# Aggregates scattered by row index where they are stored, and three sorts of single nodes moved from the last stage into the pair loop

## The chip, the cores and the metric

The kernel runs on one core of a Trainium2 chip (trn2). The metric is device time in microseconds (us), the median of the runs timed. A profile is one execution of its own; engines are called PE (TensorE, matrix products), DVE (VectorE), ACT (ScalarE), POOL (GpSimd) and SP (SyncE, which here only issues DMAs). L1380 is line 1380 of the kernel before.

## What is computed

Sixteen graphs of 1024 nodes with 64 channels go through two layers. Layer 0, after a layer norm and a ReLU, removes some edges of each node (by their rank) and takes, over the neighbours left and for each channel by itself, three quantiles; their weighted sum is the node's aggregate. A two-layer perceptron and a residual follow. Layer 1 is three graph convolutions with the full adjacency and a last linear layer. The part that matters here, cut:

```python
nd = adj_d > 0                                    # neighbours left, with the node itself
vals = jnp.where(nd[..., None], x[:, None, :, :], jnp.inf)
s = jnp.sort(vals, axis=2)
nv = nd.sum(2)
for tau, w in zip(TAUS, WTS):                     # 0.25, 0.5, 0.75
    pos = tau * jnp.maximum(nv - 1, 0)
    ...
    agg = agg + w * (v_lo + frac * (v_hi - v_lo))
out = x + agg
h = relu(out @ W1 + b1);  y = h @ W2 + b2          # layer 0
...
x1 = bn(relu(adj @ (h @ W) + b))                   # layer 1, three times
```

## The kernel before

**Pairs.** Graphs go in eight pairs; graph x of pair p is 2p + x. Rows of the tiles are the 64 channels of both graphs, or 128 nodes.

**Places.** `prepare_one` computes a graph's edges left and the number of neighbours of each node. Nodes are ranked by that number: `place` (L906) holds for every node its rank, so that nodes with few neighbours come first and one sorting network of fixed size serves a whole range of places. Rows of edges are sent to DRAM at their place by eight indirect DMAs of POOL (L914, `live_d`) and loaded back in that order (L929, `lp`). `find_live` and `list_rows` make from them what the sorts need.

**Two kinds of sort.** Places 0 to 639 (three blocks), 960 to 1007 (MID) and 1008 to 1023 (TAIL) are gathered by PE (`gather_block`: masks `s` made by DVE at L1170 or L1235, products at L1195 or L1266, ACT takes them out of PSUM) and sorted with channels on partitions. Places 640 to 959 are the single nodes (`NODES`, kinds 0, 1 and 2, with 17, 19 and 21 slots): `fetch_nodes` has POOL ask for each slot's rows with an indirect DMA (L1380, two per slot), and `sort_nodes` sorts them with nodes on partitions. Every sort is a network of DVE minima and maxima (L1111), then products (L1123) and sums (L1132). A sort of kinds 0 and 1 is for the two graphs of one pair, one of kind 2 for two pairs. `NODE_ORDER` lists the 20 sorts; `fetch_next` takes the next one of it and gives its rows a buffer (`gn` if nothing else is said). An ask waits for the DVE instruction that stood last in the program when it was written (L1387).

**Storing.** An aggregate of a block is turned by PE (L1292), copied by ACT into `o` (two buffers) and sent to `agg_d` of its graph at its places by ACT's DMA queue (L1302). One of single nodes is sent by SP's queue (L1426, L1429). `send` and `send_nodes` do this for what is waiting.

**Order.** `weave` interleaves, by hand-set shares, a sort with the steps of other generators. Each turn p of the pair loop (L1789) sorts pair p while `prepare` of pair p + 1 goes on (`SHARES`: how many of its steps go to each sort of the turn): block 0, a sort of single nodes, block 1, block 2, a second sort of single nodes, the MID places, and in turn 4 the TAIL places of four pairs. So 14 of the 20 sorts of single nodes are done in the loop's seven turns. The last pair is sorted in the late stage (L1821), with the six that are left, and there the steps of `later` are woven in (`LATE_SHARES`): for each pair, the rest of layer 0 (`first_layer`) and layer 1 (`next_layer`), the next pair's `first` between the steps of this pair's `second`. `done.sent` is the number of pairs whose aggregates are on their way.

**Loading.** `later` needs aggregates by node, while `agg_d` holds them by place. So `load` gathers them with sixteen indirect DMAs of POOL per pair (L1573), one per 128 nodes of each graph, by `place`. They go ahead of other work as the scheduler sees it (`high_priority`), but on POOL's queue instructions run in the order in which they stand. The tile `agg` is a single buffer. DVE's first instruction on it is L1470.

Of the kernel before, what the change touches and what calls it, by code (L numbers as in the profile page):

```python
# [14 lines left out]
I32 = mybir.dt.int32  # L15
# [17 lines left out]
SHARES = (20, 22, 14, 30, 9)  # L33
LATE_SHARES = (8, 8, 8, 8, 9, 9, 10, 8, 11, 8, 8)
# [11 lines left out]
    ((0,), 0), ((0,), 1), ((1,), 0), ((1,), 1), ((0, 1), 2), ((2,), 0), ((2,), 1), ((3,), 0), ((3,), 1), ((2, 3), 2),  # L46
    ((4,), 0), ((4,), 1), ((5,), 0), ((5,), 1), ((4, 5), 2), ((6,), 0), ((6,), 1), ((6, 7), 2), ((7,), 0), ((7,), 1),
# [27 lines left out]
REST = 960  # L75

# [332 lines left out]
def graph_layers_kernel(ctx: ExitStack, tc: tile.TileContext, ins, out: bass.AP):  # L409
# [80 lines left out]
    nc.gpsimd.iota(node_i, pattern=[[P, NT]], base=0, channel_multiplier=1)  # L490
    node = const.tile([P, NT], F32, name="node")
# [141 lines left out]
    agg_d = [dram.tile([N, C], F32, name=f"agg_d{b}") for b in range(NB)]  # L633
    live_d = [dram.tile([N, N // 4], I32, name=f"live_d{b}") for b in range(NB)]
# [149 lines left out]
    def prepare_one(st, x, pools, ahead=None):  # L784
# [5 lines left out]
        edge = work.tile([P, NT, N], F8, tag="byte", bufs=4, name="edge")  # L790
# [8 lines left out]
        for t in range(NT):  # L799
            a, coming = coming, load(t + 1) if t + 1 < NT else None  # L800
            nc.scalar.activation(  # L801
                edge[:, t, :], a[:, :].bitcast(U32), AF.Sign, accum_out=found[:, 0, b, t : t + 1], saturate=False
            )
            one = work.tile([P, N], F8, tag="one", bufs=2, name="one")
            nc.vector.tensor_scalar(one, a, 1.0, None, ALU.is_equal, saturate=False)  # L805
            pt = ps.tile([P, NT, P], F32, tag="big", bufs=2, name="ptE")
            for u in range(NT):
                nc.tensor.matmul(  # L808
                    out=pt[:, u, :], lhsT=one[:, u * P : (u + 1) * P], rhs=ident_h, start=True, stop=True
                )  # L810
            nc.scalar.activation(  # L811
                edgeT[:, :, t * P : (t + 1) * P], pt, AF.Copy, accum_out=found[:, 1, b, t : t + 1], saturate=False
            )
            yield
# [48 lines left out]
        for t in range(NT):  # L863
            q = ps.tile([P, N], F32, tag="big", bufs=2, name="q")
            for hf in range(NH):
# [19 lines left out]
                edge[:, t, :], q, AF.Relu, bias=bias(-2.0), accum_out=nv[:, t : t + 1], saturate=False  # L885
# [4 lines left out]
        nc.vector.scalar_tensor_tensor(key, nv, float(N), node, ALU.mult, ALU.add)  # L890
        minus = work.tile([P, NT], F32, tag="minus", name="minus")
# [32 lines left out]
        def fetch():  # L924

            lp = work.tile([P, NT, N // 4], I32, tag="byte", bufs=4, name="lp")
            for t in range(0, NT, 4):
                with tc.high_priority():
                    load = nc.gpsimd.dma_start(  # L929
                        out=lp[:, t : t + 4, :],  # L930
                        in_=live_d[b][t * P : (t + 4) * P, :].rearrange("(t p) n -> p t n", p=P),
                    )
                for sent in rows_sent:
                    tc.add_manual_dep(
                        load.ins, sent.ins.name,
                        mybir.DependencyInfo(mybir.DependencyClass.Sync, mybir.DependencyReason.DATA),
                        reason="rows sent by place",
                    )
            return lp[:, :, :].bitcast(F8)

        def find_live(lp_all, listed):
# [12 lines left out]

            half = slice(x * C, (x + 1) * C)
# [330 lines left out]

    def store(p, agg, cols, place0, pools, after=None):
# [13 lines left out]
        for x in range(2):  # L1301
            nc.scalar.dma_start(out=agg_d[2 * p + x][place0 : place0 + n, :], in_=o[:n, x * C : (x + 1) * C])  # L1302
# [64 lines left out]
    def fetch_nodes(pairs, i, pools, tag):  # L1367
# [4 lines left out]
        pool = work if tag == "s" else keep if tag == "r0" else rows  # L1372
        g = pool.tile([P, slots, G * C], F32, tag=tag, bufs=2 if tag == "s" else 1, name="g_nodes")
# [45 lines left out]
    def send_nodes():  # L1419

        for pairs, i, agg in waiting_nodes:
            j0, j1, _, _ = NODES[i]
            for a in range(agg.shape[1] // C):
                cols = slice(a * C, (a + 1) * C)
                if i < 2:
                    nc.sync.dma_start(out=agg_d[2 * pairs[0].p + a][j0:j1, :], in_=agg[:, cols])  # L1426
                else:
                    for x in range(2):
                        nc.sync.dma_start(  # L1429
                            out=agg_d[2 * pairs[a].p + x][j0:j1, :], in_=agg[x * C : (x + 1) * C, cols]  # L1430
                        )
# [124 lines left out]
    def later(pools, keep, done):  # L1556
# [4 lines left out]
        def load(p):  # L1561
# [5 lines left out]
            for x in range(2):  # L1567
# [3 lines left out]
                with tc.high_priority():  # L1571
                    for t in range(NT):
                        nc.gpsimd.indirect_dma_start(  # L1573
                            out=agg[:, t, x, :],
                            out_offset=None,
                            in_=agg_d[b][:, :],
                            in_offset=bass.IndirectOffsetOnAxis(ap=place[:, b, t : t + 1], axis=0),
                        )
# [184 lines left out]
    with ExitStack() as stack:  # L1763
# [6 lines left out]
        with ExitStack() as inner:  # L1770
# [18 lines left out]
            for p in range(NP - 1):  # L1789
# [3 lines left out]
                def steps(n):  # L1793
                    return ahead, SHARES[n], 0.0, 1.0

                weave(sort_block(st, 0, pools), gather_block(st, 1, pools), asking(nodes, 0.0, 0.9), steps(0))
                weave(sort_nodes(nodes, pools), gather_block(st, 2, pools), steps(1))
                nodes = fetch_next()
                weave(sort_block(st, 1, pools), asking(nodes, 0.1, 1.0, 0.4), steps(2))
                send_nodes()  # L1800
                both = rows_of_pairs(MID, p, p + 1, p, pools, "g1")
                weave(
                    sort_block(st, 2, pools), gather_block(st, MID, pools, into=both),
                    gather_block(st, MID + 1, pools, (early[0], "a", 2)), asking(nodes, 0.0, 0.7), steps(3),
                )
                if p in TAILS:
                    tails = rows_of_pairs(MID + 1, *TAILS[p], TAILS[p][1], pools, "g0")
                weave(sort_nodes(nodes, pools), steps(4))
# [12 lines left out]
        with ExitStack() as inner:  # L1821
# [5 lines left out]
            def steps(n):  # L1827
# [6 lines left out]
            then = [fetch_next("r0")]  # L1834
            weave(sort_block(st, 1, pools), asking(nodes, 0.0, 0.9), steps(2))
            send_nodes()
            both = rows_of_pairs(MID, NP - 1, NP, NP - 1, pools, "g1")
            weave(
                sort_block(st, 2, pools), gather_block(st, MID, pools, into=both), asking(then[0], 0.0, 0.9), steps(3)
            )  # L1840
            tails = rows_of_pairs(MID + 1, *TAILS[NP - 1], NP - 1, pools, "g0")
            weave(sort_nodes(nodes, pools), gather_block(st, MID + 1, pools, into=tails[:, :, -TW:]), steps(4))
            then += [fetch_next(), fetch_next("s"), fetch_next("s")]
            weave(
                sort_pairs(MID + 1, *TAILS[NP - 1], tails, pools), asking(then[1], 0.0, 0.5), asking(then[2], 0.5, 1.0),
                steps(5),
            )
            send(pools)
            done.sent = NP - 2
            weave(sort_nodes(then[0], pools), asking(then[3], 0.0, 1.0), steps(6))  # L1850
            send_nodes()
            weave(sort_pairs(MID, NP - 1, NP, both, pools), steps(7))
            send(pools)
            weave(sort_nodes(then[1], pools), steps(8))
            send_nodes()
            done.sent = NP - 1
            weave(sort_nodes(then[2], pools), steps(9))
            send_nodes()
            weave(sort_nodes(then[3], pools), steps(10))
# [52 lines left out]
```

## Time and profile before

| what | value |
|---|---|
| timed runs, median of 3 (lowest, highest) | 3202.37 us (3199.89, 3215.75) |
| the profiled execution's own time | 2820.77 us |
| its span, first to last instruction | 2819.0 us |
| mean granted clock of PE | 0.871 |
| preparation of the first pair | 0 to 213.7 us |
| pair loop, seven turns | 213.7 to 1995.1 us |
| late stage | 1995.1 to 2819.0 us |
| POOL, asks for rows of single nodes (L1380) | 744, 968.6 us busy |
| POOL, gathers of aggregates (L1573) | 128, 134.0 us busy |
| POOL, scatters of edge rows (L914) | 128, 178.3 us busy |

A row of a group of instructions reads: line, engine, operation, output<-inputs, shapes, count | busy us, mean ns of one | idle time of the engine just before them and what ended most of it. Durations come from the profiled execution, which is 382 us shorter than the median of the timed runs.

### The profile page before, as it was taken

Reading aid. Unit: us, or ns where it says so; the run is one execution under the profiler, and the core shown is the slowest. Engines: PE = TensorE matmul, PEld = TensorE weight load, DVE = VectorE, ACT = ScalarE, POOL = GpSimd, SP = SyncE. Lnnn points to the kernel's source line nnn. Section 1 sums busy time; section 2 is a strip of 40 time slices with the busy share of each in tenths; the row PEclk is TensorE's granted clock in tenths of the full one; section 3 lists DMA queues with packets and bytes.
Section 4 is the critical chain, followed back from the end, with each engine's and each line's share of the span. In section 5 each row is a group of like instructions: output and inputs, shape, how many; then the busy total and the mean of one; then the engine's idle time right before and its main releaser. Section 6 shows DMA issues by size and latency. Waiting matters only on the chain. (4 is left out here: it accounts for less than half of the span.)

```text
span 2819.0 us, 54552 instructions
## 1 busy us (share of the span) xinstructions
PE 2124.0 (75%) x21226; PEld 1366.3 (48%) x21226; DVE 2260.5 (80%) x5356; ACT 1660.1 (59%) x3325; POOL 1359.1 (48%) x1171
## 2 busy tenths in 40 slices
PE   3658976996898699779746986997689496448868
PEld 2435554563555466455524553654355363234445
DVE  3137998999999899989999999999688486647943
ACT  4795877678587768868673777687423141122222
POOL 7125554375345427534625274175636748852220
PEclk9779998997998899699978987998798798778989
DMA  4214222232422323242521322322311251221211
GB/s 128 75 49 124 76 71 73 87 91 64 117 74 72 77 83 92 55 124 59 106 46 47 94 86 64 112 76 64 81 19 30 65 83 52 43 58 43 53 52 47
DMA packets 261483, 205.28 MB, mean 73 GB/s; under 512 B 217568, under 2 KB 217696, under 8 KB 257120
## 3 DMA queue, kind: packets, MB, share of 16 engines
q1 hardware_dynamic: 169216, 131.76, 15.9%
q0 software_dynamic: 40192, 62.24, 9.1%
q10 hardware_dynamic: 51808, 7.71, 2.0%
q8 instruction: 168, 2.75, 0.4%
q14 instruction: 99, 0.81, 0.1%
HBM read 148.82 MB, written 52.75 MB: 72 GB/s over the span
## 5 line engine op out<-in xcount | busy, mean ns | idle before, releaser
L1380 POOL DMA_INDIRECT g_nodes<-rows_d,rows_listed x744 | 968.6, 1302 | 951.7 <-DVE prod L1123 282.6
L1195 PE MATMUL pg<-s,hp 128*64 128x496 fp8e4 (+5 forms) x8064 | 742.2, 335 | 128.9 <-ACT hp L716 47.4
L1195 PEld LDWEIGHTS <-hp 128*64 128x64 bf16 x8064 | 445.1, 113 | 370.4 <-ACT hp L716 67.5
L1528 PE MATMUL pg<-adjT,xw 128*64 128x512 fp8e4 x2304 | 280.9, 393 | 22.9 <-ACT xw L1517 12.4
L914 POOL DMA_INDIRECT live_d<-edge,place x128 | 178.3, 1393 | 162.2 <-DVE place L906 125.9
L1170 DVE TENSOR_SCALAR s<-r 128x3200 uint16<-128x3200 uint16 (+2 forms) x192 | 199.4, 1048 | 44.5 <-PE pg L1195 44.3
L1573 POOL DMA_INDIRECT agg<-agg_d,place x128 | 134.0, 1047 | 197.1 <-DMA agg_d<-agg_nodes 117.3
L1528 PEld LDWEIGHTS <-xw 128*64 128x64 bf16 x2304 | 135.2, 113 | 151.5 <-issue 21.6
L1199 ACT ACTIVATE g<-pg 128x400 f32<-128x400 f32 (+3 forms) x168 | 84.2, 501 | 183.4 <-PE pg L1195 153.4
L801 ACT ACTIVATE edge<-a 128x1024 fp8e4<-128x1024 uint32 x128 | 135.5, 1060 | 93.0 <-DMA a<-in_adj 92.4
L1111 DVE TENSOR_TENSOR t<-g 128x800 f32<-128x800 f32 (+9 forms) x184 | 168.3, 928 | 2.1
L884 ACT ACTIVATE edge<-q,bias 128x1024 fp8e4<-128x1024 f32 x128 | 142.2, 1112 | 42.6 <-PE q L879 42.6
L903 ACT ACTIVATE stays<-keys,minus 128x1024 fp8e4<-128x1024 f32 x128 | 143.7, 1123 | 39.0 <-PE keys L895 34.9
L857 ACT ACTIVATE stays<-cs,back 128x1024 f16<-128x1024 f32 x128 | 138.8, 1114 | 47.3 <-DVE look L838 28.7
L1111 DVE TENSOR_TENSOR g<-t 128x992 f32<-128x992 f32 (+7 forms) x176 | 160.0, 934 | 2.3
L949 PE MATMUL pt<-ident_h,lp 128*128 128x128 bf16 x1024 | 106.3, 273 | 61.9 <-ACT liveT L952 36.2
L1470 DVE TENSOR_TENSOR agg<-agg,h_late 128x1024 f32<-128x1024 f32 x8 | 9.8, 1230 | 177.1 <-DMA agg<-agg_d,place 177.1
L1266 PE MATMUL pg<-s,hp 128*64 128x384 bf16 (+14 forms) x1872 | 149.2, 301 | 2.6 <-DVE s L1235 2.6
L808 PE MATMUL ptE<-ident_h,one 128*128 128x128 bf16 x1024 | 83.2, 231 | 78.5 <-DVE one L805 43.8
L811 ACT ACTIVATE edgeT<-ptE 128x1024 fp8e4<-128x1024 f32 x128 | 130.5, 1030 | 16.3 <-PE ptE L808 14.5
L1532 ACT ACTIVATE xT<-pg,c_L_gnn_b 128x512 f32<-128x512 f32 x48 | 32.9, 686 | 181.5 <-PE pg L1528 173.3
L805 DVE TENSOR_SCALAR one<-a 128x1024 fp8e4<-128x1024 f32 x128 | 89.5, 704 | 53.9 <-DMA a<-in_adj 42.6
(255 smaller groups left out, 5067.7 us busy)
## 6 DMA issues: line engine op xcount, KB each, us to landing
a<-in_adj SPq DMA_DIRECT2D x128, 512.0 KB
adjT_d<-edgeT SPq DMA_DIRECT2D x16, 1024.0 KB
lp<-live_d POOLq DMA_DIRECT2D x32, 512.0 KB
adjT<-adjT_d SPq DMA_DIRECT2D x16, 1024.0 KB
g_nodes<-rows_d,rows_listed POOLq DMA_INDIRECT x744
room<-in_x SPq DMA_DIRECT2D x16, 256.0 KB
h_d<-room SPq DMA_DIRECT2D x16, 256.0 KB
rows_d<-room SPq DMA_DIRECT2D x64, 64.0 KB
```

Of the source, the lines that this page charges most:

```text
L801: nc.scalar.activation(edge[:, t, :], a[:, :].bitcast(U32), AF.Sign, accum_out=found[:, 0, b, t : t + 1], saturate=False)
L857: nc.scalar.activation(stays[:, t, :], cs, AF.Abs, bias=back[:, t : t + 1], scale=2.0)
L884: nc.scalar.activation(edge[:, t, :], q, AF.Relu, bias=bias(-2.0), accum_out=nv[:, t : t + 1], saturate=False)
L903: nc.scalar.activation(junk, keys, AF.Sign, bias=minus[:, t : t + 1], accum_out=above[:, t : t + 1], saturate=False)
L914: sent = nc.gpsimd.indirect_dma_start(out=live_d[b][:, :], out_offset=bass.IndirectOffsetOnAxis(ap=place[:, b, t : t + 1], axis=0), in_=ed ...
L1111: sorted_by[0] = nc.vector.tensor_tensor(view(bufs, o, n1, n2), view(bufs, a, n1, n2), view(bufs, b, n1, n2), ALU.max if op else ALU.min)
L1170: nc.vector.tensor_scalar(s[:, j, :, us, :], st.r[0][:, :, us, j0:j1], abs(k - 3), 0x0808, ALU.logical_shift_right if k > 3 else ALU.logic ...
L1195: summed = nc.tensor.matmul(out=pg[x * C : (x + 1) * C, those, :], lhsT=st.hp[:, part, x, u, :], rhs=picked, start=(i == 0 and part == 0), ...
L1266: summed = nc.tensor.matmul(out=pg[x * C : (x + 1) * C, ks, w0:], lhsT=st.hp[:, part, x, u, :], rhs=s[:, ks, x, u, w0:], start=(whole and ...
L1380: asked = nc.gpsimd.indirect_dma_start(out=g[:, k, a * C : (a + 1) * C], out_offset=None, in_=rows_d[st.p][:, :], in_offset=bass.IndirectO ...
L1528: nc.tensor.matmul(out=pg[cs, :], lhsT=part[:, u, cs], rhs=adjT[x][:, u, sl], start=(u == 0 and k == 0), stop=(u == NT - 1 and k == len(xw ...
L1573: nc.gpsimd.indirect_dma_start(out=agg[:, t, x, :], out_offset=None, in_=agg_d[b][:, :], in_offset=bass.IndirectOffsetOnAxis(ap=place[:, b ...
```

## The change

**Scatter.** Four bytes are added to each row of edges: the number of the node in the pair (0 to 2047, `own_row`). They travel with the row to its place, so that after loading, `node_of` holds for each place the node that has it; three small SP DMAs per graph bring the numbers of places 896 to 959, 960 to 1007 and 1008 to 1023 to partitions where they are wanted. `agg_d` is now one tensor for a pair, by node. All stores of aggregates are indirect DMAs of POOL (`scatter`), 19 a pair: two for each stored block, two for each sort of kind 0 or 1, and one per pair for kind 2. Different scatters of a pair do not wait for each other. `load` fetches `agg` with two plain SP DMAs, which wait for all scatters of that pair.

**Order of the sorts.** Turns 1, 3 and 5 of the loop have a third sort of single nodes. Its rows have the buffer `g1`, free once block 1 is sorted, and are asked for during the sort of block 2; in these turns the MID and TAIL places are gathered beside the last sort of single nodes rather than beside block 2. The late stage keeps three of the six: kind 2 of pairs 6 and 7, and kinds 0 and 1 of pair 7. `SHARES`, `LATE_SHARES` and `NODE_ORDER` follow. `done.sent` becomes 7 once the TAIL places are stored.

```diff
-SHARES = (20, 22, 14, 30, 9)
-LATE_SHARES = (8, 8, 8, 8, 9, 9, 10, 8, 11, 8, 8)
+SHARES = ((20, 22, 14, 0, 30, 9), (20, 22, 14, 16, 14, 9))
+LATE_SHARES = (6, 6, 8, 8, 6, 16, 8, 7)
 NODE_ORDER = (
-    ((0,), 0), ((0,), 1), ((1,), 0), ((1,), 1), ((0, 1), 2), ((2,), 0), ((2,), 1), ((3,), 0), ((3,), 1), ((2, 3), 2),
-    ((4,), 0), ((4,), 1), ((5,), 0), ((5,), 1), ((4, 5), 2), ((6,), 0), ((6,), 1), ((6, 7), 2), ((7,), 0), ((7,), 1),
+    ((0,), 0), ((0,), 1), ((0, 1), 2), ((1,), 0), ((1,), 1), ((2,), 0), ((2,), 1), ((2, 3), 2), ((3,), 0), ((3,), 1),
+    ((4,), 0), ((4,), 1), ((4, 5), 2), ((5,), 0), ((5,), 1), ((6,), 0), ((6,), 1), ((6, 7), 2), ((7,), 0), ((7,), 1),
 )
...
-    agg_d = [dram.tile([N, C], F32, name=f"agg_d{b}") for b in range(NB)]
-    live_d = [dram.tile([N, N // 4], I32, name=f"live_d{b}") for b in range(NB)]
+    agg_d = [dram.tile([2 * N, C], F32, name=f"agg_d{p}") for p in range(NP)]
+    live_d = [dram.tile([N, N // 4 + 1], I32, name=f"live_d{b}") for b in range(NB)]
...
+        nc.vector.tensor_copy(edge[:, :, N:].bitcast(I32), own_row[:, x, :, None])
...
+            nc.vector.tensor_copy(node_of[:, b, :NT, None], lp_all[:, :, N:].bitcast(I32))
+            for to, first, end in (
+                (nodes_of[x * C : (x + 1) * C, st.p : st.p + 1], 0, C),
+                (node_of[: MID_END - REST, b, NT : NT + 1], C, C + MID_END - REST),
+                (node_of[: N - MID_END, b, NT + 1 :], C + MID_END - REST, P),
+            ):
+                nc.sync.dma_start(out=to, in_=node_of[first:end, b, NT - 1 : NT])
...
+    def scatter(p, rows, data):
+
+        sent = nc.gpsimd.indirect_dma_start(
+            out=agg_d[p][:, :], out_offset=bass.IndirectOffsetOnAxis(ap=rows, axis=0), in_=data, in_offset=None
+        )
+        for other in agg_sent[p]:
+            tc.declare_no_dep(sent.ins, other.ins, reason="aggregates of different nodes")
+        agg_sent[p].append(sent)
...
         for x in range(2):
-            nc.scalar.dma_start(out=agg_d[2 * p + x][place0 : place0 + n, :], in_=o[:n, x * C : (x + 1) * C])
+            at = place0 // P + (place0 >= REST) + (place0 >= MID_END)
+            scatter(p, node_of[:n, 2 * p + x, at : at + 1], o[:n, x * C : (x + 1) * C])
...
-                    nc.sync.dma_start(out=agg_d[2 * pairs[0].p + a][j0:j1, :], in_=agg[:, cols])
+                    b = 2 * pairs[0].p + a
+                    scatter(pairs[0].p, node_of[:, b, j0 // P : j0 // P + 1], agg[:, cols])
...
-                with tc.high_priority():
-                    for t in range(NT):
-                        nc.gpsimd.indirect_dma_start(
-                            out=agg[:, t, x, :],
-                            out_offset=None,
-                            in_=agg_d[b][:, :],
-                            in_offset=bass.IndirectOffsetOnAxis(ap=place[:, b, t : t + 1], axis=0),
-                        )
+                load = nc.sync.dma_start(out=agg[:, :, x, :], in_=rows_of(agg_d[p][x * N : (x + 1) * N, :]))
+                for sent in agg_sent[p]:
+                    tc.add_manual_dep(
+                        load.ins, sent.ins.name,
+                        mybir.DependencyInfo(mybir.DependencyClass.Sync, mybir.DependencyReason.DATA),
+                        reason="aggregates of all nodes",
+                    )
...
                 weave(sort_nodes(nodes, pools), gather_block(st, 2, pools), steps(1))
+                more = fetch_next("g1") if p % 2 else None
                 nodes = fetch_next()
                 weave(sort_block(st, 1, pools), asking(nodes, 0.1, 1.0, 0.4), steps(2))
                 send_nodes()
+                if more is not None:
+                    weave(
+                        sort_block(st, 2, pools), asking(more, 0.0, 0.9), asking(nodes, 0.1, 0.9, 0.2), steps(3)
+                    )
+                    weave(sort_nodes(more, pools), asking(nodes, 0.0, 0.8), steps(4))
+                    send_nodes()
                 both = rows_of_pairs(MID, p, p + 1, p, pools, "g1")
-                weave(
-                    sort_block(st, 2, pools), gather_block(st, MID, pools, into=both),
-                    gather_block(st, MID + 1, pools, (early[0], "a", 2)), asking(nodes, 0.0, 0.7), steps(3),
+                small = (
+                    gather_block(st, MID, pools, into=both), gather_block(st, MID + 1, pools, (early[0], "a", 2)),
                 )
+                if more is None:
+                    weave(sort_block(st, 2, pools), *small, asking(nodes, 0.0, 0.7), steps(4))
+                    small = ()
...
-                weave(sort_nodes(nodes, pools), steps(4))
+                weave(sort_nodes(nodes, pools), *small, steps(5))
...
-            then += [fetch_next(), fetch_next("s"), fetch_next("s")]
-            weave(
-                sort_pairs(MID + 1, *TAILS[NP - 1], tails, pools), asking(then[1], 0.0, 0.5), asking(then[2], 0.5, 1.0),
-                steps(5),
-            )
+            weave(sort_pairs(MID + 1, *TAILS[NP - 1], tails, pools), steps(5))
             send(pools)
-            done.sent = NP - 2
-            weave(sort_nodes(then[0], pools), asking(then[3], 0.0, 1.0), steps(6))
+            done.sent = NP - 1
+            weave(sort_nodes(then, pools), steps(6))
             send_nodes()
             weave(sort_pairs(MID, NP - 1, NP, both, pools), steps(7))
-            send(pools)
-            weave(sort_nodes(then[1], pools), steps(8))
-            send_nodes()
-            done.sent = NP - 1
-            weave(sort_nodes(then[2], pools), steps(9))
-            send_nodes()
-            weave(sort_nodes(then[3], pools), steps(10))
             send(pools)
```

## Prediction, on record before the result

> **What bounds the kernel now.** I read the page's rows of busy time first, then busy time in chosen stretches, then the waits of each engine, then the order of time on GpSimd (POOL).
>
> The page's first part; then, from the answer on stretches, two of the seven turns of the pair loop and the late stage (the loop's first and last turns begin and end where `hp` is finished; columns: length, then busy us and count of PE, PEld, DVE, ACT, POOL, then granted clock, DMA share, GB/s):
>
> ```profile
> PE 2124.0 (75%) x21226; PEld 1366.3 (48%) x21226; DVE 2260.5 (80%) x5356; ACT 1660.1 (59%) x3325; POOL 1359.1 (48%) x1171
> ```
>
> ```profile
> 720.00:970.00 250.00, 202.81 (x2236) 132.40 (x2232) 237.13 (x537) 188.70 (x385) 120.18 (x93) 0.90 0.29 83
> 970.00:1220.00 250.00, 209.54 (x2220) 134.62 (x2218) 228.46 (x533) 185.33 (x366) 113.99 (x92) 0.87 0.28 82
> ...
> 1995.10:2819.00 823.90, 587.86 (x4815) 368.95 (x4815) 534.36 (x1107) 201.82 (x448) 396.78 (x329) 0.84 0.24 52
> ```
>
> There are two regimes. In a loop turn (213.7 to 1995.1, seven turns of 254 us) VectorE is busy 228 to 237 of 250 us: it is the bound, TensorE next with 203 to 210. In the late stage nothing is: of 824 us DVE works 534, PE 588. The waits of that stage say why:
>
> ```profile
> DVE agg L1470 <- DMA agg<-agg_d,place: 177.1, 8, 59.3
> ...
> POOL agg L1573 <- DMA agg_d<-agg_nodes: 117.3, 2, 59.2
> ```
>
> Eight times, once a pair, VectorE stands at L1470 until the gather of the aggregates has landed, 177.1 us in all. POOL in order of time at the longest of them (DVE's last earlier instruction began at 2440.05, L1470 at 2499.59) shows that the DMA's data were not what was late:
>
> ```profile
> 2474.58 0.95 POOL L1380 DMA_INDIRECT g_nodes<-rows_d,rows_listed  x1 [0.30 <-issue]
> 2475.83 0.94 POOL L1380 DMA_INDIRECT g_nodes<-rows_d,rows_listed  x1 [0.30 <-issue]
> 2477.08 0.95 POOL L1380 DMA_INDIRECT g_nodes<-rows_d,rows_listed  x1 [0.30 <-issue]
> 2478.33 0.95 POOL L1573 DMA_INDIRECT agg<-agg_d,place  x1 [0.30 <-issue]
> ...
> 2497.10 0.94 POOL L1573 DMA_INDIRECT agg<-agg_d,place  x1 [0.30 <-DMA agg<-agg_d,place]
> ```
>
> (The reader is to see a queue without a pause: one instruction every 1.25 us, first node rows asked for, then sixteen gathers, 20 us of issue in themselves.) POOL's queue, not its data, holds up VectorE, and with it TensorE, whose granted clock fell to 0.69 in the stretch 2417 to 2515.
>
> **Removed: the gathers.** The 128 at L1573 and the node rows queued ahead of them leave that path. `agg` comes by two SP DMAs a pair. SP issues the like of it (`xt<-in_x`) in 0.4 to 3.0 us, median 0.9, and its data wait on nothing but the free tile (the same wait as now) and the scatters of that pair. For pairs 0 to 3 these were sent long before, for 5 and 6 while pair 4 is worked on. Pairs 4 and 7 may still wait: tails sorted late, eight scatters of 1.25 us and a landing of about 2.4 us (the last gather of the final chain took 2.37), some 12 us for pair 4 if nothing covered it. I leave 12 us of the 177: -165. Bounds: -177 and -100 (if SP's waits in order give a third back).
>
> **Moved: three node sorts** (pairs 4 and 5 with kind 2, pair 6 with kinds 0 and 1 drop out of the late stage; by the new order one more sort falls into turns 1, 3 and 5). The late stage has two sorts of each kind, so half of its rows is one of each. The eight L1111 groups on `t_nodes` and `g_nodes` there are 39.2, 33.4, 22.3, 18.4, 17.3, 16.6, 12.5 and 10.3: 170.0 us for 318 instructions. The product rows are 6.3 + 4.9 + 2.4 + 1.7 = 15.3 us. Half is 92.7 us busy, less the 0.08 us by which neighbours overlap (0.28 long, 0.20 apart) on some 172 instructions: 79 us.
>
> Out of the late stage they are not worth 79. Without its stalls it is 824 - 177 = 647 us; less 79 it would be 568, but PE's 588 us, at the 0.96 that its fullest stretches reach (35.66 of 37, 51.87 of 56), need 612, and the last pair's chain stands alone, some 10 to 15 us more. So PE is late next, at about 625. With 12 us of waits left, 637: the stage gains 187. I take -182.
>
> In the loop they meet the engine that is the bound: +79 in full. Bounds: +40, if DVE's 13 to 22 us of slack a turn takes part of each, and +90.
>
> **Moved with them: POOL's work.** The loop takes 114 asks of the three sorts, at 1.306 us mean there plus 0.30 between two: 183 us over three turns. Added: 152 scatters (19 a pair), of which some 130 in the loop. None is in the trace of before; the nearest row is the scatter L914, 1.39 us mean over the whole run and 1.45 in the loop, so about 1.7 us apiece: 32 us a turn, +24 instructions against the 128 gathers gone. Here a rule of the Trainium skill speaks against the change: "DMA: Bandwidth & Descriptors", Issuing engine by pattern, has simple stores on the Sync queue, and calls the hardware queues generally faster. These stores left from ACT and SP in 0.34 and 0.38 us (L1302, L1426, medians). By that rule alone 152 stores at 1.7 us, 258 us, replace 160 at about 0.4, and all would count: +190. But the row that decides is POOL's: 114 to 120 us busy of a 250 us turn. A normal turn swallows 32 us more.
>
> A turn with three sorts is another matter: 114 asks (183 us), 16 `live_d` (28), 4 `lp` (5) and about 20 scatters (34) are 250 us, in a turn of 254 + 26. And they can't be spread: `gn` is one buffer, so nothing is asked for while its sort runs (POOL waited 282.6 us on DVE's L1123 in the loop), and `g1` comes free only when block 1 is sorted. Between then and the sort of those rows lie some 40 asks, 64 us, beside a sort of block 2 that has now 16 preparation steps and no gathers, 45 us by the stretch 1087 to 1139 (50 us busy with 30 steps and the gathers). I take 20 us of standing a turn, +60; bounds 0 (an ask costs 1.25 us, as above, where VectorE stands idle) and +105.
>
> **Small ones.** ACT's copy into `o` (2 buffers) waits for scatters instead of its own DMAs; up to four stores come at once, so two copies may wait some 5 us, and PE's PSUM tiles behind ACT with them. ACT has 60 us free a turn: +5 in all, bounds 0 and +40. Behind POOL's new wait for `o` and `agg_nodes` stand asks and `live_d`; counted above. SP gets 48 tiny loads of `node_of`, waiting on a DVE copy; behind them are the next `in_x` and `h_again`. +3, bounds 0 and +10. `live_d` rows grow from 1024 to 1028 bytes; DMA is 0.28 to 0.30 busy in a turn, and a few per cent more is hidden: 0. Steps given to other phases do the same work.
>
> **Sum**, against the profiled 2820.8 us (span 2819.0 and 1.8 around it): -182 + 79 + 60 + 8 = -35, so 2786. The median of the timed runs, 3202.4, is 381.6 above, 13.5%, and no view shows where. Stretched evenly, -35 is -40. If in the timed runs PE is the slower part (at 203 to 210 us it needs some 20% to fill a turn), the sorts and POOL's lag lie partly behind it: half of 139 leaves -182 + 70 + 8 = -104, of which slower phases take perhaps a third of the gain at the stalls (55): about -50 to -60. I forecast 3202 - 52 = 3150.
>
> **Rivals.**
> - POOL becomes the bound of the odd turns (slower). It stands for s us in each of three; -182 + 79 + 8 + 3s turns positive at s = 32. For it: 250 us of queue in a 280 us turn with a dead time of 35 us at each sort. Against: DVE standing makes asks cheaper by a fifth. At s = 45, +40, stretched +45: 3247.
> - The stall comes back in another queue (no change): `agg` behind scatters, `h_late` and `out` on SP in order. With 105 of the 177 recovered: -122 + 147 = +25, or about 0 with half of POOL's lag hidden: 3202. Against: `h_late`, on the same queue, was there before L1470 each time.
> - The sorts are nearly free in the loop (much faster), PE being the slower part in timed runs, and late PE warmer than 0.84, so that its 588 us shrink by 5%: -182 - 30 + 40 + 30 + 8 = -134, stretched less: about 3085. For it: stalls let the clock fall to 0.69. Against: DVE is 94% busy in a profiled turn.
>
> **Chances.** Forecast (3110 to 3186) 0.40; much faster 0.28; no change within 0.5% (16 us, about what a measurement of this kernel can tell) 0.14; slower 0.18. Faster is 0.68. The range, 3065 to 3235, runs from beyond the much faster case's centre to short of s = 45.
>
> **What would show it.** Right: L1470's wait under 25 us in all and the late stage near 640 us; turns 1, 3 and 5 longer by 35 to 50 us than the even ones, those unchanged within 8; a DVE wait of about 20 us ahead of the moved sort's first L1111, put down to DMA `g_nodes`. Wrong: late stage above 700, L1470 waiting on SP's `agg`, ACT waiting on DMA `agg_d<-o` for tens of us, or even turns longer by over 15.

## The result, and the profile after

| | before | changed |
|---|---|---|
| timed runs, median of 4 (lowest, highest) | 3201.13 us (3183.36, 3215.75) | 3230.18 us (3225.19, 3251.55) |
| ratio | | 1.0102, 95% interval 1.0067 to 1.0137 |
| profiled execution | 2820.77 us | 3230.03 us |

The change makes the kernel about 1% slower, where 52 us of gain were forecast. The kernel before took 3183 to 3216 us in two of the six comparisons of this study (this one is the first) and 2813 to 2836 us in the four others, so that its profile of 2820.77 us is of "the level of 2830" and this profile of the changed kernel of "the level of 3200".

Busy time of each engine in the changed kernel, the page's first part:

```profile
PE 2274.2 (70%) x21207; PEld 1412.2 (44%) x21226; DVE 2257.3 (70%) x5388; ACT 1670.9 (52%) x3325; POOL 1421.7 (44%) x1196
```

VectorE does the same 2260 us of work as before in a span that is longer: it stands more. From the answer on stretches (turn 2, turn 3, the late stage; turns are cut where VectorE's last sum of the MID sort ends; columns as in the prediction):

```profile
920.80:1207.70 286.90, 207.72 (x1991) 124.29 (x1988) 220.77 (x529) 181.40 (x359) 128.85 (x106) 0.81 0.24 70
1207.70:1575.30 367.60, 253.48 (x2434) 150.90 (x2436) 266.62 (x609) 195.37 (x398) 196.00 (x157) 0.77 0.22 60
2551.40:3228.30 676.90, 579.45 (x4727) 369.29 (x4723) 448.49 (x909) 191.05 (x395) 163.20 (x132) 0.91 0.24 56
```

The late stage was cut about as forecast (677 us, 637 were said). PE is busy 579 us of it, at a granted clock of 0.91, and is now the fullest engine there. In the turns VectorE, the bound before (237 of 250), is busy 221 of 287 and 267 of 368 us. So something has come between. Its waits, in the same profile (total, times, longest):

```profile
POOL agg_d L1304 <- ACT o L1324: 241.9, 15, 80.8
DVE node_of L961 <- DMA lp<-live_d: 233.7, 16, 30.9
...
POOL agg_d L1304 <- DVE agg_nodes L1145: 103.7, 9, 25.0
...
DVE agg L1494 <- DMA agg<-agg_d: 4.8, 2, 2.6
```

The last line answers to the 177.1 us of L1470 in the kernel before: the stall for aggregates is gone. The second is new: VectorE stands 233.7 us at sixteen copies of `node_of` that take 0.17 us each. GpSimd (first and third line) now waits for those who make the data it scatters.

### The profile page after: what moved, and what is told of

Read it like the earlier page. It is cut to its first block, busy times and chain, and to the rows that moved or that the text cites. A ratio compares the mean times of both kernels' runs of the same rounds, so it can differ in the third digit from the quotient of the medians.

```text
span 3228.3 us, 54484 instructions
## 1 busy us (share of the span) xinstructions
PE 2274.2 (70%) x21207; PEld 1412.2 (44%) x21226; DVE 2257.3 (70%) x5388; ACT 1670.9 (52%) x3325; POOL 1421.7 (44%) x1196
## 5 line engine op out<-in xcount | busy, mean ns | idle before, releaser
L1405 POOL DMA_INDIRECT g_nodes<-rows_d,rows_listed x744 | 983.5, 1322 | 971.8 <-DVE prod L1136 375.4
L1208 PE MATMUL pg<-s,hp 128*64 128x496 fp8e4 (+5 forms) x8064 | 843.7, 346 | 321.2 <-issue 179.9
L1208 PEld LDWEIGHTS <-hp 128*64 128x64 bf16 x8064 | 477.4, 115 | 629.9 <-issue 313.0
L1183 DVE TENSOR_SCALAR s<-r 128x3200 uint16<-128x3200 uint16 (+2 forms) x192 | 199.5, 1046 | 217.3 <-remote 132.2
L1304 POOL DMA_INDIRECT agg_d<-o,node_of x112 | 160.1, 1429 | 272.7 <-ACT o L1324 241.9
L1279 PE MATMUL pg<-s,hp 128*64 128x384 bf16 (+14 forms) x1872 | 179.6, 325 | 73.9 <-issue 47.8
L920 POOL DMA_INDIRECT live_d<-edge,place x128 | 136.1, 1063 | 194.3 <-DVE place L912 157.1
L816 ACT ACTIVATE edgeT<-ptE 128x1024 fp8e4<-128x1024 f32 x128 | 130.4, 1024 | 83.1 <-remote 57.7
L961 DVE COPY node_of<-lp 128x8 int32<-128x8 int32 x16 | 2.8, 173 | 233.7 <-DMA lp<-live_d 233.7
L958 ACT ACTIVATE liveT<-pt 128x1024 fp8e4<-128x1024 f32 x128 | 126.8, 1029 | 68.8 <-PE pt L955 33.8
L1279 PEld LDWEIGHTS <-hp 128*64 128x64 bf16 x1872 | 106.8, 126 | 108.7 <-issue 77.9
## 6 DMA issues: line engine op xcount, KB each, us to landing
lp<-live_d POOLq DMA_DIRECT2D x32, 514.0 KB
```

What stands on the lines that cost most here:

```text
L920: sent = nc.gpsimd.indirect_dma_start(out=live_d[b][:, :], out_offset=bass.IndirectOffsetOnAxis(ap=place[:, b, t : t + 1], axis=0), in_=ed ...
L1183: nc.vector.tensor_scalar(s[:, j, :, us, :], st.r[0][:, :, us, j0:j1], abs(k - 3), 0x0808, ALU.logical_shift_right if k > 3 else ALU.logic ...
L1208: summed = nc.tensor.matmul(out=pg[x * C : (x + 1) * C, those, :], lhsT=st.hp[:, part, x, u, :], rhs=picked, start=(i == 0 and part == 0), ...
L1279: summed = nc.tensor.matmul(out=pg[x * C : (x + 1) * C, ks, w0:], lhsT=st.hp[:, part, x, u, :], rhs=s[:, ks, x, u, w0:], start=(whole and ...
L1304: sent = nc.gpsimd.indirect_dma_start(out=agg_d[p][:, :], out_offset=bass.IndirectOffsetOnAxis(ap=rows, axis=0), in_=data, in_offset=None)
L1405: asked = nc.gpsimd.indirect_dma_start(out=g[:, k, a * C : (a + 1) * C], out_offset=None, in_=rows_d[st.p][:, :], in_offset=bass.IndirectO ...
```

## The experiments

All ratios are to the kernel before in the same comparison. Spans by stage, all at the level of 2830 (us, from the profiles; "odd" is turns 1, 3 and 5 together, "even" is 2, 4 and 6):

| kernel | to the end of turn 0 | odd turns | even turns | late stage | span | ratio (95%) |
|---|---|---|---|---|---|---|
| before_again | 473.9 | 737.2 | 802.2 | 813.1 | 2826.4 | 1 |
| after_again | 514.0 | 1041.0 | 907.5 | 639.7 | 3102.2 | 1.094 (1.091 to 1.097) |
| after_late | 473.3 | 1001.1 | 793.4 | 638.7 | 2906.5 | 1.028 (1.025 to 1.031) |
| third_plain_b | 473.1 | 870.6 | 794.4 | 649.1 | 2787.2 | 0.987 (0.982 to 0.991) |
| order_only | 474.9 | 967.2 | 769.5 | 733.1 | 2944.7 | 1.044 (1.040 to 1.048) |
| scatter_late | 475.2 | 739.8 | 809.9 | 713.1 | 2738.0 | 0.969 (0.966 to 0.972) |

**The kernel before, profiled again.**

> The kernel before, unchanged, to see what its ordinary execution looks like: its first profile lasted 2820.8 us, its timed runs 3183 to 3216. Theory 1 (that profile was an unusually quick execution): this one lasts about 3200 us, its TensorE idle time put down to 'issue' is some hundreds of us (40.6 at L1195 in the first profile, 313.0 in the changed kernel's), and the loop, 1781 us in the first profile, is the longer part. Theory 2 (the profile was ordinary, and the timed runs differ for a reason outside the trace): about 2820 again, with 'issue' as small as before.

2828.15 us, and at L1195, the products that gather rows for the block sorts, about as little `issue` as in the first profile (40.6 us). (`issue` is idle time in which an engine waited for nothing that the profile shows.)

```profile
PEld L1195 <- issue: 44.6, 112, 11.1
```

Its timed runs beside it took 2813 to 2835. That is theory 2: the level goes with the comparison, not with the single execution. Each comparison was made on one chip, and no chip is known to have shown both levels; but each slow one was met once only, so that the chip as the cause is likely and not shown. Two further profiles met the quick level too (2823.93 and 2828.04 us), so no profile of the kernel before at the level of 3200 exists.

> The kernel before, unchanged, a third profile. It has been timed at 3201, 2828, 2831 and 3200 us in four comparisons, but profiled only where it takes 2820 to 2828. Theory L (where it takes 3200, TensorE's instructions come slower): if this comparison is at the level of 3200, TensorE's idle time put down to 'issue' at L1195 is above 150 us (44.6 at the level of 2828) and a turn of the loop is 30 to 50 us longer than the 245 to 256 of the quicker level. If it is at the level of 2830, as in the earlier profiles.

> The kernel before, unchanged, once more for a profile at the level of 3200 us, which none has shown yet. Theory L: if this comparison is at that level, TensorE's idle time put down to 'issue' at L1195 is above 150 us and a loop turn 30 to 50 us longer than at the other level. If it is at the level of 2830, as in the earlier profiles.

**The halves apart.** `scatter_only` is the change with the old order of sorts and shares, `order_only` the new order with the old stores and gathers.

> The scatter alone: aggregates stored by node, loaded plainly, with the order of sorts and the shares of before. Theory A (the copy of node_of and GpSimd's waits on scatters cost more than the gathers' 165 us): slower than before by 0 to 100 us, 3200 to 3300. Rival C (what costs is the third sort in the odd turns): faster than before by 100 us or more, at most 3100.

> The new order of sorts alone: stores by place and gathers as before, third sorts in turns 1, 3 and 5. Theory A: the late stage still stands for its gathers, fewer asks ahead of them; between 60 us faster and 40 slower than before, 3140 to 3240. Rival C (the third sorts cost more in the loop than they free): slower than before by 60 us or more, 3260 or above.

2977.99 us, ratio 1.054 (1.051 to 1.057), and 2949.55 us, 1.044 (1.040 to 1.048). Each half alone makes the kernel slower. For the scatter theory A has the direction right, but its +150 us lie beyond the 100 allowed; for the order rival C is right (+122 us). `order_only` still has the gathers (127.2 us of waiting at L1470), yet its late stage is 80 us shorter; its odd turns are 230 us longer.

**The copy of node_of.** First it was given to ScalarE:

```diff
-            nc.vector.tensor_copy(node_of[:, b, :NT, None], lp_all[:, :, N:].bitcast(I32))
+            nc.scalar.copy(node_of[:, b, :NT, None], lp_all[:, :, N:].bitcast(I32))
```

> The changed kernel with the copy of node_of made by ScalarE, right behind its last copy of liveT, instead of VectorE. Theory A (head of line: 16 copies on VectorE's queue stand before their rows have landed, 233.7 us in the profile of after, and everything behind them stands too): the wait vanishes from VectorE and the time falls by 80 to 200 us, to 3030 to 3150. Rival B (VectorE would have stood anyway for TensorE or GpSimd in those places): within 20 us of 3230, and the wait turns up under another name.

3089.58 us, ratio 1.093 (1.089 to 1.098). That it lies in theory A's range of 3030 to 3150 is luck, since that range was set for the level of 3200: the changed kernel itself, measured later at the level of 2830, has 1.094, and nothing was gained. The wait turned up on the other engine:

```profile
ACT node_of L961 <- DMA lp<-live_d: 338.4, 16, 32.4
```

So not the engine was wrong but the place. In the program's text the copy follows the transposes of `lp`; in the queue the scheduler had put it well ahead of them; it depends on nothing but the load. The profile of `after_again` in order of time shows one of the sixteen, VectorE and GpSimd together and below them TensorE's next use of `lp` (start, us, engine, line, what; in brackets the idle time before it):

```profile
998.77 0.96 POOL L920 DMA_INDIRECT live_d<-edge,place  x1 [0.30 <-DMA live_d<-edge,place]
1000.03 0.98 POOL L1405 DMA_INDIRECT g_nodes<-rows_d,rows_listed  x1 [0.30 <-DMA live_d<-edge,place]
1001.32 0.96 POOL L1405 DMA_INDIRECT g_nodes<-rows_d,rows_listed  x1 [0.30 <-issue]
1002.28 1.62 POOL L935 DMA_DIRECT2D lp<-live_d  x2
...
1008.00 0.17 DVE L961 COPY node_of<-lp 128x8 int32<-128x8 int32 x1 [30.50 <-DMA lp<-live_d]
1008.08 1.15 DVE L1248 TENSOR_SCALAR s<-r 128x480 bf16<-128x480 bf16 x5
...
1046.17 0.61 PE L955 MATMUL pt<-ident_h,lp 128*128 128x128 bf16 x8
```

VectorE stands at the copy from 977.5. The last of that graph's eight scatters of edge rows (L920) leaves GpSimd's queue at 999.7, `lp` is asked for at 1002.3 and has landed at 1008. TensorE turns `lp` only at 1046. Masks (L1248) that need nothing of all this stand 30 us behind a copy of rows whose other use is 38 us away. In the turns the first graph of each pair costs 22 to 31 us of waiting, the second 11 to 13.

Then the copy was put behind the last use of the same rows, on ScalarE, where it has nothing to wait for:

```diff
-                nc.scalar.activation(liveT[:, :, t * P : (t + 1) * P], pt, AF.Copy, saturate=False)
+                turned = nc.scalar.activation(liveT[:, :, t * P : (t + 1) * P], pt, AF.Copy, saturate=False)
...
-            nc.vector.tensor_copy(node_of[:, b, :NT, None], lp_all[:, :, N:].bitcast(I32))
+            named = nc.scalar.copy(node_of[:, b, :NT, None], lp_all[:, :, N:].bitcast(I32))
+            tc.add_manual_dep(
+                named.ins, turned.ins.name,
+                mybir.DependencyInfo(mybir.DependencyClass.NoSync, mybir.DependencyReason.SCHED_ONLY),
+                reason="behind the rows' own use",
+            )
```

> The changed kernel, unchanged, beside the kernel before on one chip, since the kernel before took 3201 us in the first comparison and 2828 in the second. Theory T (there the issue of TensorE's instructions was slower, and its slowness covered most of what the change costs; scatter_only at +5.4% and order_only at +4.3% are the true size of the parts): where the kernel before takes 2828 us this one takes 3030 to 3130, a ratio of 1.07 to 1.11, and where it takes 3200 about 3230. Rival (the ratio belongs to the kernel, whatever the level): 1.01 on any level.

> The changed kernel with the copy of node_of made by ScalarE and told to stand behind the last liveT copy of that graph, whose own rows were turned by TensorE long before, so that it waits for nothing. (In node_of_act the copy still stood 25 us ahead of the first use of lp, and its wait was 338.4 us on ScalarE.) Theory A (the early copy is what costs): the wait at L961 is under 5 us in all, and the time is 130 to 280 us below after_again. Rival B (only a cover for other waits): within 40 us of after_again.

> after_late once more. Theory L: at the level of 3200 a ratio of 0.97 to 1.0 (the changed kernel itself was 1.010 there and 1.094 at the level of 2830); at the level of 2830 1.028 as before. Rival (no dependence): 1.028 on both.

`after_again` 3098.81 us (ratio 1.094, as theory T has it), `after_late` 2910.00 us: 189 us less, and the copies wait for nothing. In the table all of it is in the preparation and the turns (-41, -40, -114), none in the late stage. `after_late_b` gave 1.0285 (1.024 to 1.033), again at the level of 2830, so it says nothing on the other level.

Why only 40 us in the odd turns? The copies waited as long there (118 us) as in the even ones (120 us). But while VectorE stood at a copy, GpSimd went on asking for rows. With the copies out of the way, another wait grows, first `after_again`, then `after_late`:

```profile
DVE node_of L961 <- DMA lp<-live_d: 298.9, 16, 30.5
DVE t_nodes L1124 <- DMA g_nodes<-rows_d,rows_listed: 98.2, 9, 18.2
```

```profile
DVE t_nodes L1129 <- DMA g_nodes<-rows_d,rows_listed: 168.9, 11, 26.0
```

In the third sorts of the odd turns alone it goes from 54 to 130 us. The two stalls had covered each other, so what each is worth depends on which is taken away first.

> The scatter alone, with the order of sorts of before, and the copy of node_of behind the last liveT copy. scatter_only was 150 us slower than before. Theory A (its cost was the early copy, 281.6 us of wait at L961, and the late stage gains what the gathers cost, some 140): faster than before, by 20 to 120 us on the level of 2828. Rival B (GpSimd's waits for ScalarE's o and VectorE's agg_nodes, with live_d and lp behind them, are the cost): still slower than before by 60 us or more.

> scatter_late once more. Theory L (the slower level lets less of a shortened wait be seen, since TensorE is late next): at the level of 3200 a ratio of 0.98 to 0.995, at the level of 2830 0.966 to 0.972 as before. Rival (the ratio doesn't depend on the level): 0.969 on both.

With the same edit the scatter alone takes 2739.25 us: 3.1% faster than before (second comparison 0.973, 0.969 to 0.976), 239 us below `scatter_only` (another comparison at the same level). Its turns are those of the kernel before (+10 us in six), its late stage 100 us shorter. GpSimd's waits on `o` and `agg_nodes`, which looked large in the table of waits (32.5 and 124.8 us here), cost the loop next to nothing: rival B falls.

**The third sort of the odd turns.** Between `scatter_late` and `after_late` lies the order: +171 us, +261 in the odd turns. `after_late` at turn 1, the sorts of blocks 1 and 2 and the third sort (stretches: length, then PE, PEld, DVE, ACT, POOL), and VectorE's wait in the last two:

```profile
580.40:616.90 36.50, 32.23 (x373) 20.82 (x374) 34.80 (x55) 32.24 (x75) 29.90 (x22) 1.00 0.33 108
616.90:677.80 60.90, 36.11 (x345) 24.56 (x343) 35.38 (x60) 45.36 (x73) 47.53 (x43) 0.82 0.18 53
677.80:722.90 45.10, 3.21 (x12) 1.39 (x11) 27.07 (x73) 4.67 (x7) 30.76 (x31) 0.50 0.22 62
```

```profile
DVE t_nodes L1129 <- DMA g_nodes<-rows_d,rows_listed: 42.9, 2, 24.9
```

In the second stretch VectorE works 35 of 61 us, in the third 27 of 45, and there TensorE does 3 us of work in 45. GpSimd in order of time between them, up to the two moments when VectorE may go on:

```profile
674.07 0.95 POOL L1410 DMA_INDIRECT g_nodes<-rows_d,rows_listed  x1 [0.30 <-DMA g_nodes<-rows_d,rows_listed]
675.32 1.16 POOL L1410 DMA_INDIRECT g_nodes<-rows_d,rows_listed  x1 [0.30 <-DMA g_nodes<-rows_d,rows_listed]
676.78 1.46 POOL L1410 DMA_INDIRECT g_nodes<-rows_d,rows_listed  x1 [0.30 <-DVE coef L1150]
678.55 0.94 POOL L1410 DMA_INDIRECT g_nodes<-rows_d,rows_listed  x1 [0.31 <-issue]
...
694.77 0.94 POOL L1410 DMA_INDIRECT g_nodes<-rows_d,rows_listed  x1 [0.30 <-issue]
696.01 0.94 POOL L1410 DMA_INDIRECT g_nodes<-rows_d,rows_listed  x1 [0.30 <-issue]
```

An ask every 1.25 us, with 0.30 us between two: it looks as if the queue were the bound. The DMA engines were busy 0.18 and 0.22 of these two stretches, so they were not. To test it, `third_plain` takes the asks of that sort away:

```diff
             for k in range(slots):
+                if tag == "g1" and k > 0:
+                    if k == 1:
+                        for a in range(G):
+                            nc.sync.dma_start(
+                                out=g[:, 1:, a * C : (a + 1) * C],
+                                in_=rows_d[pairs[0].p][: P * (slots - 1), :].rearrange("(p s) c -> p s c", p=P),
+                            )
+                    yield
+                    continue
```

It leaves out the gathering of 16 of the 17 slots of these three sorts: the same bytes come from the same table, as consecutive rows.

> after_late, but the rows of the third sort of turns 1, 3 and 5 come, after the first slot, by two plain SP DMAs of the same size (they are rows of the same pair, but not the neighbours asked for), so that 32 of the 34 asks per odd turn leave GpSimd's queue; the third sort itself stays. In after_late the odd turns are some 75 us longer than in the kernel before, and VectorE stands 42.9 us in one of them for g_nodes while GpSimd issues without a pause. Theory P (GpSimd's queue bounds the odd turns): VectorE's two waits for g_nodes there go, 35 to 45 us a turn, and the ratio to before falls from 1.028 to between 0.96 and 0.99. Rival V (VectorE's own work of a third sort, 27 us busy a turn, and the preparation beside it are what is long): at most 10 us a turn, a ratio of 1.015 or above.

> third_plain once more (rows of the third sort of odd turns by two plain DMAs, not the neighbours asked for). At the level of 3200 it was 0.976. Theory P (GpSimd's queue bounds the odd turns): at the level of 2830 between 0.96 and 0.99, that is 110 to 190 us below after_late in the same comparison. Rival V (the third sort's own work): 1.015 or above, at most 40 us below after_late.

At the level of 3200: 3119.67 us, 0.976 (0.972 to 0.980). At that of 2830: 2787.07 us, 0.987 (0.982 to 0.991), 116 us below `after_late_b` in the same comparison (2902.80). Its two stretches:

```profile
613.30:649.30 36.00, 23.50 (x228) 16.73 (x228) 35.30 (x61) 29.83 (x49) 27.38 (x23) 0.90 0.23 70
649.30:676.70 27.40, 15.66 (x129) 9.22 (x129) 27.15 (x73) 20.26 (x32) 19.05 (x18) 0.69 0.30 89
```

61 and 45 us have become 36 and 27, which is VectorE's own work (35 and 27): 43 us for one turn, and 130.5 in the three, as much as the 130 us of waiting above. Theory P holds. The odd turns are still 131 us longer than those of `scatter_late`; how much of that is the third sort's own work (rival V) isn't separated.

**Buffers o.** `bufs=2` becomes `bufs=4` in the line that makes `o` in `store`, for `after_late` and for `scatter_late`.

> after_late with four buffers o instead of two. Theory A: ScalarE's wait at L1324 for scatters (61.0 us in the profile of after) goes, and the time falls by 0 to 30 us against after_late. Rival B (GpSimd's queue is what is late, and the buffers only say so): no change within 10 us.

> The version that beat both, scatter_late (ratio 0.969), with four buffers o in place of two. There ScalarE waits 99.5 us at L1329 for scatters, once for 72.5 us, and TensorE behind it. Theory A: once in the late stage this wait stands on the path; it goes, and the ratio falls to between 0.945 and 0.96. Rival B (GpSimd's queue is what is late): 0.965 to 0.972.

> scatter_late with four buffers o. At the level of 3200 it was 0.989. At the level of 2830: theory A (the 72.5 us wait of ScalarE at L1329 stands on the late stage's path) 0.945 to 0.96, rival B (GpSimd's queue is what is late) 0.965 to 0.975, the value of scatter_late.

In the changed order four buffers give 22 us (2888.25, 1.020, 1.017 to 1.022). With the old order nothing that can be told: 0.967 (0.965 to 0.970) against 0.969 and 0.973. ScalarE's wait of 72.5 us is gone from its profile and the time is the same, so it was not on the path. At the level of 3200 this version gains only 1.1% (3162.71 us, 0.989, 0.986 to 0.992), which is neither theory's value.

**The two levels.** The changed kernel once more:

> The changed kernel, unchanged. At the level of 3200 a ratio of 1.005 to 1.015, at the level of 2830 of 1.09 to 1.10: the ratio goes with the level (theory L), or it is something else that differed between the first comparison and the later one (rival).

3092.75 us, 1.094 (1.092 to 1.097) on the level of 2830, a second time; 1.010 was measured on that of 3200. The ratio goes with the level. Three kernels by stage on both levels (us, the quick level's rows of the first two as above):

| kernel at the level of 3200 | to the end of turn 0 | odd turns | even turns | late stage |
|---|---|---|---|---|
| changed (profile after) | 557.4 | 1068.6 | 925.4 | 676.9 |
| less after_again | +43 | +28 | +18 | +37 |
| third_plain | 552.8 | 956.1 | 923.3 | 685.2 |
| less third_plain_b | +80 | +86 | +129 | +36 |
| scatter_late_o4 | 547.5 | 891.7 | 942.4 | 770.5 |
| less scatter_late_o4_b | +75 | +148 | +135 | +57 |

What stands out between the levels is TensorE's wait for nothing that the profile shows; first the profile after (3200), then `after_again` (2830):

```profile
PEld L1208 <- issue: 313.0, 387, 10.1
...
PE pg L1208 <- issue: 179.9, 237, 2.6
```

```profile
PEld L1208 <- issue: 50.9, 81, 10.1
```

The two kernels without the waits at L961 pay for the slow level in their turns (+86 and +129, +148 and +135 us); the changed kernel, whose VectorE stands there anyway, pays little (+28 and +18). So at the level of 3200 most of the early copy's cost has company. That reading is argued from the table: `after_late` was never run at that level. What was measured there is the copy and the asks together: `third_plain`, without the early copy and with 2 of the 34 asks of each third sort, is 110 us below the changed kernel (3119.67 and 3230.18, in two comparisons), where at the level of 2830 it is 312 us below.

## Why the prediction was wrong, step by step

- **Removed: the gathers, -165; late stage, -182.** Right for the two together. Stage 813.1 to 639.7 us at one level, -173; the stage was said to be 637. The wait for `agg` is 4.8 us (12 was taken). That PE would be late next fits: 563 of 640 us busy in `after_again`. The scatter alone gives -100 of it, the order alone -80; the -165 as a term of its own was not measured.
- **Small ones: "SP gets 48 tiny loads of `node_of`, waiting on a DVE copy ... +3, bounds 0 and +10".** This is the step that failed. I priced who waits for the copy and not what the copy waits for. It waits for a load that waits for eight scatters of GpSimd, and it was looked for where the program's text has it, behind the transposes, not where VectorE's queue has it. Cost: 189 us at the level of 2830 (`after_late` against `after_again`), 239 in the scatter alone, against the +3 of the sum. At the level of 3200, where the forecast was made for, its cost by itself isn't known; with the early copy and nearly all asks of the third sorts gone (`third_plain`), the kernel takes 3119.67 us there, inside the forecast of 3110 to 3186.
- **POOL's lag in odd turns, +60, bounds 0 and +105.** The mechanism (one buffer, no asks during its sort, the block 2 phase too short for them) was right. In the changed kernel VectorE waits 54 us for rows in the three moved sorts at the level of 2830 and 17 at that of 3200, both within the bounds; but that is luck, because the copies' stall, which the sum did not have, covered the rest. Without it the lag is 43 us in a turn, 130.5 in three, beyond the bounds. The stretch explains it: in turn 1 of `after_late`, 616.9 to 697 us, GpSimd sent 45 asks in 60.5 us with the pauses, near the 40 in 64 that were counted. Not counted were eight scatters of edge rows, two loads of `lp` and two scatters of `o`, 19 us; and VectorE had run out of other work after 33 us, not 45. By the slower rival's own count (it decides at 32) a lag of 43 alone turns the sum. That rival's price at s = 45, +40 without stretching, stands against +76 and +79 in `after_late_b` and `after_late` (medians). "DVE standing makes asks cheaper by a fifth" came true, 1.25 us where VectorE stood against 1.31 + 0.30, and did not suffice.
- **Three sorts in the loop, +79.** Loop and preparation grow by 254 us from before to `after_late`; less 130.5 of lag and the 12 of the scatter (`scatter_late`) this leaves 112: more than 79 and beyond the bound of 90. Which part of that is the sorts and which is, for instance, the MID gathers that moved with them isn't settled.
- **The scatters in place of plain stores.** A normal turn swallowed them, as said: 12 us in the whole loop. The rule of the Trainium skill that speaks against them ("DMA: Bandwidth & Descriptors", Issuing engine by pattern), by which alone I had +190, did not decide: the scatter with the copy in its right place is 80 and 92 us faster than before in two comparisons. A scatter of `o` took 1.22 us and one of `agg_nodes` 1.74 (`after_again`), against 1.45 by the row I had taken.
- **ACT's wait for o, +5, bounds 0 and +40.** 110.0 us of waiting in `after_again`, named beforehand as a sign of being wrong, but worth only 22 (`after_late_o4`): inside the bounds.
- **From the profiled to the timed level, -52.** The sum was -35 on a profile of a level at which the change costs +276 by the spans. "If in the timed runs PE is the slower part ... the sorts and POOL's lag lie partly behind it" fits better than even stretching: +267 us (medians, `after_again`) becomes +29. But what the slow level hid is by the table above the copy's stall as well, which wasn't in the sum.
- **The signs.** Even turns "longer by over 15" was named as a sign of error, and they are: 272 against 245 in turn 2. The odd turns were to be longer than these by 35 to 50; they grew by 101 us each, the even ones by 35 (`after_again` less `before_again`). L1470 and the late stage were right.

The likeliest case, much faster and no change were all wrong. The slower rival's cause is the smaller half of what was found (116 us, `third_plain_b` below `after_late_b`), and the copy (189 us), which no case had as a cost, the larger. That this rival's 3247 us lies close to the 3230 measured, and 3230 within the outer range, is luck: the sum behind them lacks the copy.

## What to carry to other kernels

An instruction of 0.17 us is not free in an in-order queue: ask what it waits for and where the scheduler put it, not where the source has it, and pin it behind the last use of its input. When work moves into a stage, count the queue that feeds it over the stretch between "its buffer is free" and "its data are wanted", not over the whole turn. Stalls cover each other: taking away 298.9 us of waiting was worth 189, because the next wait grew. And when profile and timed runs differ by 13%, treat them as two sources: this change was 1% slower at one level and 9% at the other, as argued above because its stall fell together with TensorE's slow issue.

## What the runs showed of the hardware that was not expected

- The same program ran at two levels 13% apart, each steady to about 1%. On the slow level TensorE's time without a visible wait at L1208 was 493 us in the changed kernel (313.0 and 179.9), against 50.9 for the weight loads on the quick one, with the granted clock 0.82 and 0.84. Over all lines, matrix products stood 277 to 297 us for `issue` in the three profiles of the slow level that are named above, and at most 3 us in their counterparts on the quick one. In stretches of it, as 1046 to 1066 us of the profile after, TensorE issued 18 products in 20 us, one or a few at a time, between 1050 and 1058 us with pauses of 0.34 to 0.36 or 1.58 to 1.74 us. Why is open.
- Waits of GpSimd at its scatters, 157 us in `scatter_late`, cost the loop next to nothing; of VectorE's 298.9 us at L961 in `after_again` 189 were time.
- `live_d` rows of 1028 bytes instead of 1024 cost GpSimd nothing that can be seen: the scatters of them took 1.28 us each in `scatter_late`, whose turns are otherwise like those before, and 1.38 in `before_again`.
